# A fused decoder layer on one core: which engine sums, multiplies, normalizes and writes out at the end

## The chip, the core and the metric

The kernel runs on one core of a Trainium2 chip. Its time is the device time of one execution in microseconds (us); the number that counts is the median of the timed executions. Each core has a matrix engine (TensorE, PE in the profile; PEld is its weight load), a vector engine (VectorE, DVE), a scalar engine (ScalarE, ACT), GpSimd (POOL) and SyncE (SP), which here issues nearly all DMAs. Every engine takes its instructions in the order in which the program lists them, and waits at an instruction until the semaphores that it names are set.

## The reference

The input `x` has 4 sequences of 1024 tokens with 512 features. All numbers are 32-bit floats.

```
x = x + gated_self_attention(layernorm(x))     # 16 heads of 32; softmax, gated per query and key, renormalized
x = x + cross_attention(layernorm(x), ctx)     # 16 heads of 32; keys and values from 1024 tokens of 384 features
x = x + ffn(layernorm(x))                      # 512 -> 64, each of the 64 through its own 16-unit relu network, 64 -> 512
```

Softmax is `exp(s) / sum(exp(s))`. The kernel forms `exp(s)` unnormalized, sums `exp(s) * v` and `exp(s)` separately, and multiplies the first by the reciprocal of the second at the end. The layernorm has no weights: it is `(x - mean) * rs` with `rs = 1 / sqrt(var + eps)`.

## The kernel before

**Units.** The work is cut into 8 units: u = 0 to 3 are self-attention (`ph == 0`) on the four sequences, u = 4 to 7 are cross-attention (`ph == 1`). The last unit is u = 7. A unit has two halves (`hf`) of 512 queries, a half has four groups (`g`) of four heads, and a group has eight steps (`kt`), one for each 128 keys. `attention(u, hf)` makes the 32 steps of a half.

**A step.** `scores` multiplies keys by queries (L623) into PSUM and ScalarE takes the exponential (L629) into two tiles `e`, each of two heads by 512 queries (128x1024). There are six `e` buffers, so three steps are in flight. VectorE then adds the tiles of the eight steps into `es` (L646 for the first sum, L648 for the others). After that the step before is finished: `times` multiplies `e` by the values into the PSUM tile `av` (L671).

**Two ways to the sums of exponentials.** Where `shared` holds, VectorE adds only the first of a step's two `e` tiles, and TensorE sums the second with a column of ones into the PSUM tile `sm` (L679, at each odd step for two steps). Where it does not hold, VectorE adds both tiles and TensorE has no L679. `shared` holds in the self-attention units and in the last unit; units 4 to 6 do without it.

**The end of a group.** `normalize` copies `av` (L688), and with `shared` also `sm` (L690), into the single buffer `both`. One step later `add_up` sums the partitions of `es` by ones (L701), ScalarE copies the result (L702), and SyncE writes it to memory and reads it back in another layout (L707 to L717). `divide` forms the reciprocals (L738), writes them to memory (L741) and reads them back broadcast as `recb` (L745). `multiply` (L751) multiplies `both` by `recb` into the query tile `q`. `after(steps, f, behind)` sets the step: in the last unit `divide` comes three steps after `add_up` and `multiply` three steps after that, so a group's `multiply` is in step 7 of the next group. With `behind` the call comes after that step's scores and additions, without it ahead of them. The next group's `av` copy needs `both`, so it needs this `multiply`. The very last group (`closing`) has a path of its own.

**Beside the steps.** `run` spreads other work over the 32 steps by cost. In the last unit (`beside`, branch `u + 1 == n`) the half `hf` carries what follows the half before it: the output projection (`project`, L106, with L845, L849, L850 behind it on VectorE) in groups 0 and 1, the statistics' root on GpSimd (`root`), the normalization into a tile `r2` (`norm`, L319) and its way to memory (`away`, L323) at the start of group 2, the reading back as `xn` (`load_xT`, L328), the 64 inner features (`inputs`, L937), and then the 16 relus (`hidden`). `r2` has two buffers, so the third normalization of a half waits until the first one's rows have been written. Two normalizations follow step 0 of group 2 and two follow step 1. `hidden` forms a relu on VectorE (L989) where `own` holds and on ScalarE (L993) where it does not; the sum over the 16 units is on VectorE (L1000). The outputs (`outputs`) are two products (L1011) each, two additions of the residual on VectorE (L1019) and two DMAs on SyncE (L1021). The projection of the half before, for its first token tile and last group, is placed right after step 7 of group 0.

**Score buffers.** Scores go through two PSUM tiles of two banks and, in the last unit, through two spare banks where nothing else needs them (`score_banks`). So the scores of half a step can start when the exponentials three half steps back are done.

**The tail.** After the last step the program goes on in an order written out by hand: the last group's sums, the projection, the normalization, the feed-forward network and the last four output tiles.

Of the kernel before, what the change touches and what calls it, by code (L numbers as in the profile page):

```python
# [10 lines left out]
F32 = mybir.dt.float32  # L11
# [5 lines left out]
P = 128  # L17
# [51 lines left out]
def moderate_path(tc: tile.TileContext, a: dict, out: bass.AP, flag: bass.AP):  # L69
    nc = tc.nc  # L70
    x = a["x"]
    with ExitStack() as st:
# [527 lines left out]
        def attention(u, hf):  # L600
# [5 lines left out]

            shared = ph == 0 or u + 1 == len(order)

# [6 lines left out]
            def scores(g, kt):  # L615
# [16 lines left out]
                if closing(g):  # L632
# [9 lines left out]
                    return es  # L642
                for i in range(1 if shared else 2):
                    if kt == 1:
                        me.setdefault("es", {})[i] = p1.tile([P, 2, HALF], F32, tag=f"es{i}", name="es")
                        nc.vector.tensor_tensor(me["es"][i], me["e", 0][i], es[i], ALU.add)  # L646
                    elif kt > 1:
                        nc.vector.tensor_tensor(me["es"][i], me["es"][i], es[i], ALU.add)  # L648
# [19 lines left out]
            def times(g, kt, es):  # L668
                for h in range(HG):
                    r = slice(h * DH, (h + 1) * DH)  # L670
                    nc.tensor.matmul(  # L671
                        av[r, :], lhsT=me["v"][:, kt, HG * g + h, :], rhs=es[h // 2][:, h % 2, :],
                        start=(kt == 0), stop=(kt == NT - 1),
                    )
                if shared and kt % 2 and not closing(g):

                    for j in range(4):
                        t, h = kt - 1 + j // 2, j % 2
                        nc.tensor.matmul(  # L679
                            sm[j * DH : j * DH + sums, :],  # L680
                            lhsT=me["sw"][:, t, HG * g + 2 + h, :] if ph == 0 else ones, rhs=me["e", t][1][:, h, :],
                            start=(kt == 1), stop=(kt == NT - 1),
                        )

            def normalize(g):
                i = (u * 2 + hf) * HG + g
                both = p1.tile([P, 3, HALF], F32, tag="both", name="both")
                nc.scalar.copy(both[:, 0, :], av)  # L688
                if shared:
                    nc.scalar.copy(both[:, 1, :], sm)  # L690
# [7 lines left out]
            def add_up(g, i, both, added):  # L698
# [8 lines left out]
                nc.sync.dma_start(s1[0:n], rows[0:n, 0, 2, :])  # L707
                if not shared:
                    nc.sync.dma_start(c[:, 0, 0, :], s1[0:n].rearrange("h (q e) -> (h q) e", e=INNER))
# [12 lines left out]
            def divide(g, i, both, c):  # L722
                if shared:
                    both_ = p2.tile([P, sums, INNER], F32, tag="c2", name="both_")
                    nc.vector.tensor_tensor(both_, c[:, 0:sums, 0, :], c[:, 0:sums, 1, :], ALU.add)
                else:
                    both_ = c[:, 0:1, 0, :]
# [16 lines left out]
                for j in range(HG):  # L744
                    nc.sync.dma_start(  # L745
                        all_[j * DH : (j + 1) * DH, :], rec_d[i % 4][j : j + 1, :].to_broadcast([DH, HALF])
                    )
                after(apart(g), lambda: multiply(g, both, all_), behind=u + 1 < len(order))

# [51 lines left out]
        def post(u, hf):  # L801
# [65 lines left out]
            def root(a=0, n=4):  # L867
# [4 lines left out]
                for t in range(n):  # L872
                    res["rs", a + t] = rs[:, t : t + 1]
                res["rs all"] = rs

            def shift():
# [24 lines left out]
            def norm(t):  # L901
                def f():
# [9 lines left out]
                    r2 = p2.tile([P, 1, D], F32, tag="r2", name="r2")  # L912
                    normalized(r2[:, 0, :], res[t], res["mv"], res["rs", t], t)
                    away(rows_d[b][hf], r2, t, 1)
# [67 lines left out]
            def hidden(h):  # L982
                def f():

                    own = u + 1 < n
                    if h < INNER:
# [20 lines left out]
            def outputs(t):  # L1007
# [8 lines left out]
                def add():  # L1016
                    for k in range(2):
                        i = 2 * k + t
                        nc.vector.tensor_tensor(res[i], res["po", t][k], res[i], ALU.add)  # L1019
                        tt = 4 * hf + i  # L1020
                        nc.sync.dma_start(out[b][tt * P : (tt + 1) * P, :], res[i])  # L1021
# [847 lines left out]
```

## Time and profile before

| what | us |
|---|---|
| median of 3 timed runs | 2163.8 |
| lowest and highest of them | 2163.7, 2164.66 |
| the profiled execution's own time | 2166.25 |
| its span, from first to last instruction | 2164.4 |
| TensorE busy | 2145.8 (99%) |
| VectorE busy | 1503.4 (69%) |
| ScalarE busy | 1233.1 (57%) |
| GpSimd busy | 133.0 (6%) |

The profile page gives the busy time of each engine, the chain of work that ended last, and groups of instructions by line and shape with their mean duration. The trace behind it answers questions: what waited for what, the instructions of one engine in order of time, and the busy time of each engine in a stretch. A time such as 2084.6 is counted from the first instruction. In a line of the timeline the columns are start, duration, engine, line, operation, output and inputs, shapes and count; a bracket gives the idle time of the engine before it and what ended it. The last unit's steps run from about 1918 to 2126 us.

### The profile page before, as it was taken

The page shows a single profiled execution, that of the slowest core. Times are in us where ns is not written, and L with a number is a line of the kernel's source. Part 1 is how long each engine was busy: PE and PEld are TensorE (multiplying, and loading weights), DVE is VectorE, ACT ScalarE, POOL GpSimd, SP SyncE. Part 2 cuts the span into 40 slices and gives each one's busy share as a digit, 9 for nine tenths or more (in the row PEclk, how much of TensorE's full clock was granted, in tenths as well). Part 3 has the DMA queues.
Part 4 walks back from the last instruction along what each step waited for, and adds up shares of the span by engine and source line. Part 5 has one row for each costly group of instructions (what it writes and reads, how often), then busy time and mean ns, then how long its engine had stood idle before and what let it go on. Part 6 is the DMA issues. An engine that isn't in the chain of part 4 may idle for free.

```text
span 2164.4 us, 52976 instructions
## 1 busy us (share of the span) xinstructions
PE 2145.8 (99%) x22792; PEld 555.9 (26%) x22792; DVE 1503.4 (69%) x2251; ACT 1233.1 (57%) x1495; POOL 133.0 (6%) x182
## 2 busy tenths in 40 slices
PE   9999999999999999999999999999999999999998
PEld 4322222222222222222222222222222222222223
DVE  3477675786766866657667666787878868876656
ACT  0156545655556554565666666565655566566765
POOL 2000010040120100001000010000000000000001
PEclk9999999999999999999999999999999999999999
DMA  6412134032331221211322113322423122322231
GB/s 169 122 47 68 52 100 114 19 87 69 90 109 34 81 59 53 68 48 65 71 71 79 63 59 69 96 66 71 89 80 102 63 61 57 98 60 71 71 90 47
DMA packets 154136, 161.71 MB, mean 75 GB/s; under 512 B 47002, under 2 KB 92698, under 8 KB 152740
## 3 DMA queue, kind: packets, MB, share of 16 engines
q1 hardware_dynamic: 149828, 156.14, 25.9%
q8 instruction: 180, 2.95, 0.6%
q0 software_dynamic: 2080, 0.98, 0.3%
q10 hardware_dynamic: 1984, 1.12, 0.2%
q14 instruction: 64, 0.52, 0.1%
HBM read 115.40 MB, written 42.74 MB: 73 GB/s over the span
## 4 chain that ended last, share of the span: by engine, by line
PE 97%; DVE 1%; ACT 1%; issue 1%; DMA 0%; SPq 0%; POOL 0%; DVEq 0%; ACTq 0%
PE f L106 37%; PE s L623 24%; PE av L671 23%; PE sm L679 6%; PE sm L701 3%; PE s L106 1%; PE f L937 1%; ACT e L629 1%; PE f L623 0%; PE f L1011 0%; DMA xin<-in_x 0%; PE f L498 0%; DVE res L1019 0%; PE f L971 0%; DVE es L648 0%
## 5 line engine op out<-in xcount | busy, mean ns | idle before, releaser
L629 ACT ACTIVATE e<-s 128x1024 f32<-128x1024 f32 x997 | 969.4, 1023 | 715.7 <-PE s L623 509.1
L648 DVE TENSOR_TENSOR es<-es,e 128x1024 f32<-128x1024 f32 x522 | 628.4, 1227 | 259.2 <-ACT e L629 258.4
L623 PE MATMUL s<-q,k 32*64 32x512 f32 x7976 | 583.6, 613 | 0.5 <-ACT e L629 0.4
L671 PE MATMUL av<-e,v 128*32 128x512 f32 x4096 | 551.6, 604 | 0.0
L106 PE MATMUL f<-xT,w 128*32 128x512 f32 x2816 | 333.7, 592 | 0.0
L656 DVE SCALAR_TENSOR_TENSOR eg<-e,sw,eg 128x512 f32<-128x512 f32 x448 | 315.6, 746 | 9.3 <-ACT eg L655 9.3
L646 DVE TENSOR_TENSOR es<-e 128x1024 f32<-128x1024 f32 x87 | 104.4, 1223 | 213.4 <-ACT e L629 202.6
L106 PE MATMUL f<-w,q 128*32 128x512 f32 x1984 | 238.6, 593 | 2.0 <-DVE res L845 1.8
L623 PEld LDWEIGHTS s<-q,k 32*64 32x64 f32 x7976 | 127.0, 129 | 412.4 <-ACT e L629 201.6
L671 PEld LDWEIGHTS av<-e,v 128*32 128x32 f32 x4096 | 88.4, 108 | 403.4 <-issue 403.0
L106 PEld LDWEIGHTS f<-xT,w 128*32 128x32 f32 x2816 | 92.2, 110 | 210.4 <-issue 208.0
L679 PE MATMUL sm<-e,sw 128*2 128x512 f32 x1024 | 133.3, 592 | 0.0
L106 PE MATMUL f<-w,xT 128*32 128x512 f32 x896 | 106.0, 592 | 0.6 <-DVE q L308 0.6
L106 PEld LDWEIGHTS f<-w,q 128*32 128x32 f32 x1984 | 64.9, 110 | 152.1 <-issue 143.2
L106 PE MATMUL f<-w,ctxT 128*32 128x512 f32 x768 | 92.3, 592 | 0.0
L106 PE MATMUL f<-ctxT,w 128*32 128x512 f32 x768 | 92.3, 592 | 0.0
L853 POOL TENSOR_TENSOR r<-res,bo_bc 128x512 f32<-128x512 f32 x32 | 40.9, 1278 | 759.4 <-DVE res L845 613.2
L701 PE MATMUL sm<-es,fixed 128*1 128x512 f32 x348 | 66.1, 596 | 3.5 <-ACT both L690 3.3
L314 POOL TENSOR_SCALAR rs<-fmv 128x4 f32<-128x4 f32 (+2 forms) x18 | 10.1, 562 | 854.8 <-DVE fmv L850 854.8
L845 DVE TENSOR_TENSOR res<-f,res 128x512 f32<-128x512 f32 x62 | 42.6, 687 | 27.7 <-PE f L106 15.0
L1000 DVE SCALAR_TENSOR_TENSOR g<-hid,units,g 128x256 f32<-128x256 f32 x105 | 50.3, 479 | 0.9 <-ACT hid L993 0.2
L751 DVE TENSOR_TENSOR q<-both,recb 128x512 f32<-128x512 f32 x63 | 43.2, 686 | 8.5 <-DMA recb<-rec_d 8.5
(285 smaller groups left out, 1185.6 us busy)
## 6 DMA issues: line engine op xcount, KB each, us to landing
recb<-rec_d SPq DMA_DIRECT2D x252, 64.0 KB
xT<-rows_d SPq DMA_DIRECT2D x60, 256.0 KB
rows_d<-r SPq DMA_DIRECT2D x60, 256.0 KB
w<-in_xattn_Wo SPq DMA_DIRECT2D x9, 1024.0 KB
w<-wout_d SPq DMA_DIRECT2D x8, 1024.0 KB
res<-in_x SPq DMA_DIRECT2D x32, 256.0 KB
x1b_d<-r SPq DMA_DIRECT2D x32, 256.0 KB
res<-x1b_d SPq DMA_DIRECT2D x32, 256.0 KB
```

The lines of the kernel that those rows point to most:

```text
L106: nc.tensor.matmul(to[r], lhsT=lhsT[:, j, :] if len(lhsT.shape) == 3 else lhsT[:, r], rhs=rhs, **flags)
L623: nc.tensor.matmul(two[j][m : m + 64], lhsT=k[r, g, kt * P + m : kt * P + m + 64], rhs=q[r, g, :], start=True, stop=True,)
L629: nc.scalar.activation(e[:, h, :] if len(reads) == 1 else e[:, h.start, :], s, AF.Exp, scale=SCALE)
L646: nc.vector.tensor_tensor(me["es"][i], me["e", 0][i], es[i], ALU.add)
L648: nc.vector.tensor_tensor(me["es"][i], me["es"][i], es[i], ALU.add)
L656: nc.vector.scalar_tensor_tensor(eg, es[0][:, h, :], gate(kt), eg, ALU.mult, ALU.add)
L671: nc.tensor.matmul(av[r, :], lhsT=me["v"][:, kt, HG * g + h, :], rhs=es[h // 2][:, h % 2, :], start=(kt == 0), stop=(kt == NT - 1),)
L679: nc.tensor.matmul(sm[j * DH : j * DH + sums, :], lhsT=me["sw"][:, t, HG * g + 2 + h, :] if ph == 0 else ones, rhs=me["e", t][1][:, h, :], ...
L701: nc.tensor.matmul(sm[j * DH : j * DH + 1, :], lhsT=ones, rhs=e, start=True, stop=True)
L751: nc.vector.tensor_tensor(me["q", hf][:, g, :], both[:, 0, :], all_, ALU.mult)
L845: nc.vector.tensor_tensor(r, res["po"], r, ALU.add)
L1000: nc.vector.scalar_tensor_tensor(res["g"], res["hid"], units[:, 2, h - 1 : h], res["g"], ALU.mult, ALU.add)
```

## The change

It has five parts.

1. In the last unit, group 1 of each half is no longer `shared`: VectorE adds both `e` tiles, the L679 products and the L690 copy go, `add_up` has four products in place of two, and the way through memory has two DMAs in place of four.
2. In the last unit `multiply` comes behind the scores and additions of its step.
3. In units 4 to 7, except for the last half, ScalarE normalizes the tokens in place of VectorE, with a shift `nm = -mean * rs` that GpSimd forms by two more instructions.
4. The relus of unit 6's second half go from VectorE to ScalarE.
5. Of the last four output tiles one is copied out of PSUM by ScalarE, added by GpSimd and written by a DMA that ScalarE issues.

```diff
--- before.py
+++ after.py
@@ -604,7 +604,8 @@
             steps = []
             sums = 2 if ph == 0 else 1
 
-            shared = ph == 0 or u + 1 == len(order)
+            def shared(g):
+                return ph == 0 or (u + 1 == len(order) and not (g == 1))
 
             def apart(g):
                 return 2 if u + 1 < len(order) else 3
@@ -640,7 +641,7 @@
                     if kt == 3:
                         after(2, lambda: by_ones(me["first"], True, False), behind=True)
                     return es
-                for i in range(1 if shared else 2):
+                for i in range(1 if shared(g) else 2):
                     if kt == 1:
                         me.setdefault("es", {})[i] = p1.tile([P, 2, HALF], F32, tag=f"es{i}", name="es")
                         nc.vector.tensor_tensor(me["es"][i], me["e", 0][i], es[i], ALU.add)
@@ -672,7 +673,7 @@
                         av[r, :], lhsT=me["v"][:, kt, HG * g + h, :], rhs=es[h // 2][:, h % 2, :],
                         start=(kt == 0), stop=(kt == NT - 1),
                     )
-                if shared and kt % 2 and not closing(g):
+                if shared(g) and kt % 2 and not closing(g):
 
                     for j in range(4):
                         t, h = kt - 1 + j // 2, j % 2
@@ -686,7 +687,7 @@
                 i = (u * 2 + hf) * HG + g
                 both = p1.tile([P, 3, HALF], F32, tag="both", name="both")
                 nc.scalar.copy(both[:, 0, :], av)
-                if shared:
+                if shared(g):
                     nc.scalar.copy(both[:, 1, :], sm)
                     added = [me["es"][0][:, 0, :], me["es"][0][:, 1, :]]
                     if ph == 0:
@@ -705,7 +706,7 @@
                 rows = both.rearrange("(j r) s q -> j r s q", r=DH)
                 n = len(added)
                 nc.sync.dma_start(s1[0:n], rows[0:n, 0, 2, :])
-                if not shared:
+                if not shared(g):
                     nc.sync.dma_start(c[:, 0, 0, :], s1[0:n].rearrange("h (q e) -> (h q) e", e=INNER))
                 else:
                     for k in range(sums):
@@ -720,7 +721,7 @@
                 after(apart(g), lambda: divide(g, i, both, c))
 
             def divide(g, i, both, c):
-                if shared:
+                if shared(g):
                     both_ = p2.tile([P, sums, INNER], F32, tag="c2", name="both_")
                     nc.vector.tensor_tensor(both_, c[:, 0:sums, 0, :], c[:, 0:sums, 1, :], ALU.add)
                 else:
@@ -745,7 +746,7 @@
                     nc.sync.dma_start(
                         all_[j * DH : (j + 1) * DH, :], rec_d[i % 4][j : j + 1, :].to_broadcast([DH, HALF])
                     )
-                after(apart(g), lambda: multiply(g, both, all_), behind=u + 1 < len(order))
+                after(apart(g), lambda: multiply(g, both, all_), behind=True)
 
             def multiply(g, both, all_):
                 nc.vector.tensor_tensor(me["q", hf][:, g, :], both[:, 0, :], all_, ALU.mult)
@@ -872,6 +873,10 @@
                 for t in range(n):
                     res["rs", a + t] = rs[:, t : t + 1]
                 res["rs all"] = rs
+                if ph == 1 and not last:
+                    nm = res["nm"] = p2.tile([P, n], F32, tag="ve", name="nm")
+                    nc.gpsimd.tensor_tensor(nm, res["mv"][:, a : a + n, 0], rs, ALU.mult)
+                    nc.gpsimd.tensor_scalar(nm, nm, -1.0, None, ALU.mult)
 
             def shift():
                 nm = res["nm"] = p2.tile([P, 2], F32, tag="ve", name="nm")
@@ -910,7 +915,10 @@
                             normalized(to, res[t], res["mv"], res["rs", t], t)
                         return
                     r2 = p2.tile([P, 1, D], F32, tag="r2", name="r2")
-                    normalized(r2[:, 0, :], res[t], res["mv"], res["rs", t], t)
+                    if ph == 1:
+                        nc.scalar.activation(r2[:, 0, :], res[t], AF.Identity, bias=res["nm"][:, t : t + 1], scale=res["rs", t])
+                    else:
+                        normalized(r2[:, 0, :], res[t], res["mv"], res["rs", t], t)
                     away(rows_d[b][hf], r2, t, 1)
                 return [(0, f)]
 
@@ -982,7 +990,7 @@
             def hidden(h):
                 def f():
 
-                    own = u + 1 < n
+                    own = u + 1 < n and (u + 2 < n or hf == 0)
                     if h < INNER:
                         hid = p2.tile([P, 2 * P], F32, tag="hid", name="hid")
                     if own and h < INNER:
@@ -1016,8 +1024,14 @@
                 def add():
                     for k in range(2):
                         i = 2 * k + t
+                        tt = 4 * hf + i
+                        if last and i == 2:
+                            r2 = p2.tile([P, D], F32, tag="r2", name="r2")
+                            nc.scalar.copy(r2, res["po", t][k])
+                            nc.gpsimd.tensor_tensor(res[i], r2, res[i], ALU.add)
+                            nc.scalar.dma_start(out[b][tt * P : (tt + 1) * P, :], res[i])
+                            continue
                         nc.vector.tensor_tensor(res[i], res["po", t][k], res[i], ALU.add)
-                        tt = 4 * hf + i
                         nc.sync.dma_start(out[b][tt * P : (tt + 1) * P, :], res[i])
 
                 def f():
```

## The prediction

> **What bounds the kernel now.** I read the page's busy times first, then the waits of TensorE, then the last unit's groups in a table of stretches, then the instructions around the one long wait.
>
> ```profile
> PE 2145.8 (99%) x22792; PEld 555.9 (26%) x22792; DVE 1503.4 (69%) x2251; ACT 1233.1 (57%) x1495; POOL 133.0 (6%) x182
> ```
>
> TensorE is the bound. Work taken off it counts, work taken off VectorE counts only where TensorE waits for VectorE. Its waits add up to little (columns: total, times, longest):
>
> ```profile
> PE sm L701 <- ACT both L690: 3.3, 2, 2.1
> ```
>
> Both are at the start of a half's group 3: 1.24 us at 1999.4 and 2.05 us at 2102.9. The stretches (busy time and count of each engine; PEclk is the granted clock) are group 1 of the first half, groups 1 and 2 of the second, and 3.3 us behind the longer wait:
>
> ```profile
> 1941.00:1974.00 33.00, 33.00 (x337) 8.00 (x340) 22.66 (x42) 16.98 (x19) 1.55 (x3) 1.00 0.08 26
> ...
> 2043.70:2076.70 33.00, 33.00 (x336) 7.99 (x340) 17.02 (x27) 20.43 (x31) 1.55 (x3) 1.00 0.09 26
> 2076.70:2101.70 25.00, 24.06 (x262) 5.25 (x260) 15.12 (x24) 19.29 (x28) 0.00 (x0) 1.00 0.59 161
> 2102.90:2106.20 3.30, 3.30 (x16) 0.83 (x18) 1.80 (x3) 2.29 (x3) 0.00 (x0) 0.50 0.00 0
> ```
>
> In group 1 VectorE has 10 to 16 us free and ScalarE 13 to 16. In group 2 ScalarE is the busier one. The last line: after a wait of 2.05 us TensorE ran at half clock for 3.4 us, which costs another 1.7.
>
> **Part 1, TensorE's gain.** The products by ones in group 1 (start, duration):
>
> ```profile
> 2076.64 1.06 PE L671 MATMUL av<-e,v 128*32 128x512 f32 x8
> 2077.52 1.04 PE L679 MATMUL sm<-e,fixed 128*1 128x512 f32 x8
> 2078.49 0.66 PE L623 MATMUL f<-q,k 32*64 32x512 f32 x4
> ```
>
> From L671 to the scores behind it are 1.85 us; without L679 (2073.51 to 2074.51) it is 1.00. So L679 costs 0.85 us, four times a group: 3.4 us in each of two groups, 6.8 in all. The two further products of L701 run in columns of the array that are idle beside the two of now: nothing.
>
> **Part 1, VectorE's cost.** 7 more additions in a group at 1.15 us (two in 2.35) are 8.05 us. They fit into the free time, but not at its end. Walking VectorE's list from step 5 of group 1 in the second half, with TensorE 0.85 us earlier for each L679 gone: the additions of step 6 end at 2071.35, the first output pair (L1019, 1.2 us) at 2072.55, the additions of step 7 at 2074.85, `multiply` (now behind them, 0.62) at 2075.45, the second output pair at 2076.65. Before it was 2077.02. So TensorE's 2.5 us up to here shrink to 0.4 on the path through VectorE to the output DMAs, and SyncE issues the rest behind those.
>
> **Part 3 in group 2 of the second half.** The lines on which the forecast rests:
>
> ```profile
> 2077.52 1.89 SPq L820 DMA_DIRECT2D res<-x1b_d  x4
> 2079.51 0.85 SPq L323 DMA_DIRECT2D rows_d<-r  x2
> ...
> 2082.65 1.02 ACT L629 ACTIVATE e<-s 128x1024 f32<-128x1024 f32 x1 [0.50 <-PE f L623]
> ...
> 2084.62 1.19 DVE L319 TENSOR_SCALAR r<-res,fmv,rs 128x512 f32<-128x512 f32 x2 [2.58 <-DMA rows_d<-r]
> ...
> 2097.42 1.71 SPq L745 DMA_DIRECT2D recb<-rec_d  x4
> 2100.91 0.69 DVE L751 TENSOR_TENSOR q<-both,recb 128x512 f32<-128x512 f32 x1 [1.70 <-DMA recb<-rec_d]
> 2101.68 0.59 ACT L688 COPY both<-av 128x512 f32<-128x512 f32 x1 [1.88 <-PE s L623]
> 2102.88 1.02 PE L701 MATMUL sm<-es,fixed 128*1 128x512 f32 x2 [2.05 <-ACT both L690]
> ```
>
> The third normalization waited 2.58 us on VectorE for its `r2` buffer, whose rows were issued at 2079.51, behind four loads of 256 KB, and had landed at 2084.5: 5 us. On VectorE nobody minded. On ScalarE the exponentials of step 2 (2082.65) stand behind it. New times: `av` copy 2076.7; two normalizations of 0.75 (L908, the same operation in the tail: two in 1.52) to 2078.2; exponentials of step 1 to 2080.2; L702 to 2080.8. The rows are issued at 2079.1, land 5 us later, so ScalarE stands from 2080.8 to 2084.15. The third and fourth normalization end at 2085.65, the exponentials of step 2 at 2087.6. TensorE gets half of the scores of step 3 out by 2082.7, then waits for the first of these exponentials (2086.65); its values product of step 2 starts at 2087.65, against 2085.44 before. The 3.4 us are gone and 2.2 more.
>
> But the end of group 2 had slack of the other kind. There the last four lines are the chain: `recb` lands, `multiply` frees `both`, the copies follow, L701 starts at 2102.88. In the new program the rows of the later two normalizations are issued at 2085.0 (before: 2086.69), and everything down to `recb` comes 1.3 us earlier, so TensorE is no longer held there. It needs 15.4 us from the product of step 2 to the end of the scores ahead of L701 (2085.44 to 2100.83), which puts L701 at 2103.05. A wait of 4 us should halve the clock for 3.4 us as the 2.05 us did; TensorE works for some 2.6 of these, a loss of 1.3: 2104.35. Before, the same half-clock stretch came behind 2102.88, so the place to compare with is 2102.88 + 1.7 = 2104.58. Sum for this half: -0.2 us.
>
> [...]
>
> **The same in the first half.** There no loads stand ahead of the rows (issued 1975.58), and `xn` loads show a landing 2.3 us after issue (1983.2 to 1985.55). VectorE's second output pair ends at 1975.55 (before 1974.4), `multiply` at 1974.35, so the `av` copy waits until 1974.4 and TensorE 0.35 us for it. The two pairs of normalizations put the exponentials of step 2 at 1980.6 to 1982.6, and the product of step 2 starts at 1982.65, against 1982.75: the 3.4 us are lost here as well, in waits of at most 1 us. The reciprocals' chain then comes 1.0 us earlier, `multiply` ends at 1997.0 in place of 1998.0, and L701 starts at 1998.25 in place of 1999.38. Sum: -1.2 us (1.1 and the 0.1).
>
> **Part 2.** Ahead of the additions, a `multiply` that waits for `recb` holds them; behind them it holds nothing. At the end of group 2 it buys nothing, since L701 waits for the copies too. At the end of group 0 of the second half it costs:
>
> ```profile
> 2039.29 0.68 DVE L751 TENSOR_TENSOR q<-both,recb 128x512 f32<-128x512 f32 x1
> 2040.75 1.90 PE L106 MATMUL f<-w,q 128*32 128x512 f32 x16
> 2041.03 1.22 DVE L648 TENSOR_TENSOR es<-es,e 128x1024 f32<-128x1024 f32 x1 [1.06 <-ACT e L629]
> ```
>
> The second half of those 16 products (from 2041.6) reads the `q` that L751 writes. Behind the addition L751 ends at 2042.85: TensorE waits 1.25 us, call it +1.3.
>
> **Part 4.** 16 relus leave VectorE, which has room here, for ScalarE at 0.5 us apiece (L993: 605 ns, overlapped by 0.1). They fall one to two in a step from 2003 to 2038, where ScalarE's idle time is 3.7 us in group 3 (five gaps) and 2.5 us in group 0 up to step 5, for 4 and 3 us of relus and 1.8 of copies that it has anyway. Step by step the `sm` copy ahead of L701 of group 0 ends at 2022.95 in place of 2022.2, and TensorE keeps this loss: +0.8. Bounds 0 (as in the second half's group 3, where relus already are on ScalarE and TensorE waited only 0.18) and 1.7 (all relus beyond the idle time).
>
> **Part 3 in units 4 to 6.** Five halves. TensorE leaves 1.0 to 2.0 us of idle in ScalarE's step there, and a normalization is 0.75. Twice (root ending at 1504.3 and at 1750.3) ScalarE comes to the first one before GpSimd has `nm`: a wait to about 1751.2 with two small instructions at 0.35 behind the copy. The exponentials then end at 1753.9 and TensorE needs them at 1754.12. I take +0.2 for all; bounds 0 and 1.5 (GpSimd's small operations reach 1.1).
>
> **Part 5.** Four additions from 2155.28 to 2157.76 become three, to 2157.1. The fourth tile goes by a copy (0.6) and a GpSimd addition (1.28, as L881): 2157.2. I take -0.5, bounds 0 and -0.7. It lies on the path to the end.
>
> **The sum** against the profiled execution (span 2164.4, own time 2166.25; its span is near the timed runs' median of 2163.8, to which I apply the difference): -1.2 + 0.8 + 1.3 - 0.2 + 0.2 - 0.5 = +0.4 us, so 2164.2.
>
> **Rivals.** (a) The cover holds: rows land 2.3 us after issue in the second half too, or ScalarE's queue lags less than I walked. Then the 6.8 us stay, both waits at the start of group 3 go (3.3) and with them the half-clock stretch (1.7), less 2.1 for parts 2 and 4 and 0.5 from the tail: 2163.8 - 6.8 - 3.3 - 1.7 + 2.1 - 0.5 = 2153.6. Half of it, 2158.7, is what one half gives. For it: only the second half shows a wait for `r2`, and in units 4 to 6 none did. Against: the loads of 1 MB ahead of those rows do not change.
>
> (b) Slower: rows in the first half land after 5 us as well, because the four output DMAs, 256 KB each, now lie closer to them. ScalarE then stands until 1981.1, the product of step 2 starts at 1984.65 (+1.9), the wait of 2.6 us halves the clock there too (+1.7), and L701 comes at 2.3 us behind its place of now, in place of 1.1 ahead, with the full 1.7 for the clock in the second half (+0.4 more): 2164.2 + 3.5 + 0.4 = 2168.1, and each further 0.5 us of landing adds as much. It decides from a landing of some 3 us. Against: the row of the first half shows a normalization at 1979.26 without a wait.
>
> (c) The change does less than it says: additions and norms only move, no wait appears or goes beyond the L679 saving, and the tail: 2163.8 - 6.8 - 0.5 = 2156.5. Both long waits would stay where they are; that needs the chain through memory to move with TensorE, which the walk denies.
>
> **How the numbers follow.** A measurement of this kernel can tell about 0.2% from no change, 4.3 us: faster is below 2159.5, slower above 2168.1. Forecast (within a few us of now) 0.62; (a) with its half and (c) 0.24; (b) and worse, such as ScalarE becoming the bound in group 3, 0.14. The range leaves out a tenth on each side: 2157.0 to 2168.5.
>
> **What would show it.** Right: L679 and L690 absent in group 1; L908-like normalizations on ScalarE with an idle gap of 2 to 4 us near 2081 to 2084 released by `rows_d`; TensorE waiting for exponentials there and PEclk 0.5 behind it; the wait at L701 gone; a wait of about 1.3 us of L106 for `q` near 2042; a slightly shorter end. Wrong: no such gap on ScalarE, group 1 and group 2 of a half together 3 us shorter or more.

## The result, and the profile after

The change makes the kernel slower: 2171.29 us median of 9 runs (2168.57 to 2172.6) against 2164.16 us for the kernel before, also 9 runs (2162.47 to 2166.54). The ratio is 1.0031, interval 1.0021 to 1.0041. The forecast was 2164.2 us, with a range up to 2168.5: the time lies outside it, on the slow side.

The profiled execution of the kernel after has a span of 2170.5 us (before 2164.4). The page's line of busy times:

```profile
PE 2146.5 (99%) x22736; PEld 553.4 (25%) x22736; DVE 1500.4 (69%) x2218; ACT 1258.5 (58%) x1538; POOL 142.0 (7%) x197
```

TensorE has 56 matmuls fewer on record and is still busy 0.7 us longer. The products by ones were taken out: group 1 has 1.6 us less in the first half and 2.2 in the second. The busy time came back in group 2 of the second half (3.1 us, where the clock is halved), in group 3 of the first (1.9) and in units 4 to 6 (1.4). ScalarE has 25 us more, GpSimd 9. In TensorE's waits (total, times, longest) the 3.3 us at the start of a half's group 3 have shrunk to 0.3, and two new waits have come in elsewhere:

```profile
PE s L624 <- ACT e L630: 3.1, 3, 2.8
...
PE f L106 <- DVE q L752: 1.1, 1, 1.1
...
PE sm L702 <- ACT both L691: 0.3, 1, 0.3
```

The table of stretches (busy time and count of PE, PEld, DVE, ACT, POOL, then PEclk, DMA share, GB/s) for group 1 of the first half, groups 1 and 2 of the second half, and the half-clock stretch:

```profile
1942.30:1974.20 31.90, 31.27 (x310) 7.92 (x308) 28.01 (x47) 16.96 (x19) 4.34 (x5) 1.00 0.07 23
2046.00:2077.10 31.10, 31.07 (x316) 7.66 (x308) 22.99 (x32) 20.44 (x31) 4.34 (x5) 1.00 0.08 26
2077.10:2106.90 29.80, 26.74 (x252) 5.39 (x240) 16.52 (x23) 20.51 (x29) 0.00 (x0) 0.89 0.48 135
2089.80:2096.60 6.80, 6.80 (x44) 1.03 (x40) 4.21 (x8) 4.12 (x6) 0.00 (x0) 0.50 0.84 159
```

Group 1 got shorter: 31.1 us for 33.0 in the second half. Group 2 of the second half got longer, with 3 us in which TensorE stands and 6.8 at half clock, where before it was 25.0 us with 0.9 idle. The reason is on ScalarE (start, duration, and in brackets the idle time ahead with its releaser; the first line is of unit 5, the last of the tail):

```profile
1505.46 0.81 ACT L919 ACTIVATE r<-res,nm,rs 128x512 f32<-128x512 f32 x1 [2.45 <-POOL nm L879]
...
2080.10 1.53 ACT L919 ACTIVATE r<-res,nm,rs 128x512 f32<-128x512 f32 x2
...
2086.88 1.52 ACT L919 ACTIVATE r<-res,nm,rs 128x512 f32<-128x512 f32 x2 [2.88 <-DMA rows_d<-r]
2088.30 1.00 ACT L630 ACTIVATE e<-s 128x1024 f32<-128x1024 f32 x1
...
2160.26 0.59 ACT L1030 COPY r<-s 128x512 f32<-128x512 f32 x1 [4.30 <-DVE res L1034]
```

The second pair of normalizations stands 2.88 us until the rows of the first pair have left, and the exponentials of step 2 stand behind it. SyncE's queue shows why the rows are late: they are issued at 2082.03 behind the four residual loads.

```profile
2080.03 1.90 SPq L821 DMA_DIRECT2D res<-x1b_d  x4
2082.03 0.85 SPq L323 DMA_DIRECT2D rows_d<-r  x2
...
2087.72 1.02 SPq L323 DMA_DIRECT2D rows_d<-r  x2
2090.55 1.93 SPq L328 DMA_DIRECT2D xn<-rows_d  x4
```

TensorE's own instructions show the two new waits, for the `q` of part 2 and for the late exponentials. Its matmuls take twice as long behind the second: eight of L672 took 1.06 us at 2083.67 and 1.94 at 2090.93.

```profile
2044.53 1.06 PE L106 MATMUL f<-w,q 128*32 128x512 f32 x8 [1.13 <-DVE q L752]
...
2083.67 1.06 PE L672 MATMUL av<-e,v 128*32 128x512 f32 x8
...
2089.36 1.65 PE L624 MATMUL s<-q,k 32*64 32x512 f32 x8 [2.75 <-ACT e L630]
2090.93 1.94 PE L672 MATMUL av<-e,v 128*32 128x512 f32 x8
```

Last, the program's closing instructions. Each engine ends with a DRAIN. The columns are the count, the shortest, median and longest duration in ns, and the first and last start. Kernel after:

```profile
L1879 POOLq DRAIN  x3: 46/107/5052, 2164.6 to 2170.3; - x3
L1879 SPq DRAIN  x3: 7/7/13, 2167.9 to 2170.0; - x3
```

Kernel before:

```profile
L1865 POOLq DRAIN  x3: 46/107/5052, 2154.5 to 2164.1; - x3
L1865 SPq DRAIN  x3: 7/7/13, 2163.5 to 2163.8; - x3
```

GpSimd's first drain takes 5.05 us in both. Before, it ran from 2154.5 to 2159.6 while SyncE still waited for the output DMAs until 2163.5: hidden. After, GpSimd has the last output's addition, its drain starts at 2164.6 and ends at 2169.7, 1.8 us behind SyncE's 2167.9.

**The time by stages.** The start of ScalarE's copy of `av` marks the end of each group. Set against before, less the 0.33 us that the two profiles differ at the first such copy, the shifts at the end of each stage are: 1.41 us at the end of unit 6, still 1.41 after group 0 of the last unit's first half, 0.52 after group 2, 1.26 after group 3, 2.62 after group 0 of the second half, 0.76 after group 1, 5.64 after group 2, 3.92 at the start of the tail and 5.83 at the end. The later sections use the same marks.

They compare one execution of each kernel, and the executions of one kernel differ. The two spans are 6.1 us apart, the medians 7.1: the profiled execution before (2166.25 us) is one of the longer ones.

### The profile page after: what moved, and what is told of

It reads as the page before. It is cut to its first block, busy times and chain, and to the rows that moved or that the text cites. A ratio compares the mean times of both kernels' runs of the same rounds, so it can differ in the third digit from the quotient of the medians.

```text
span 2170.5 us, 52906 instructions
## 1 busy us (share of the span) xinstructions
PE 2146.5 (99%) x22736; PEld 553.4 (25%) x22736; DVE 1500.4 (69%) x2218; ACT 1258.5 (58%) x1538; POOL 142.0 (7%) x197
## 5 line engine op out<-in xcount | busy, mean ns | idle before, releaser
L649 DVE TENSOR_TENSOR es<-es,e 128x1024 f32<-128x1024 f32 x534 | 641.9, 1227 | 277.6 <-ACT e L630 276.4
L624 PE MATMUL s<-q,k 32*64 32x512 f32 x7976 | 588.4, 613 | 3.3 <-ACT e L630 3.1
L672 PE MATMUL av<-e,v 128*32 128x512 f32 x4096 | 550.0, 605 | 0.0
L624 PEld LDWEIGHTS s<-q,k 32*64 32x64 f32 x7976 | 127.7, 129 | 418.5 <-ACT e L630 211.8
L672 PEld LDWEIGHTS av<-e,v 128*32 128x32 f32 x4096 | 87.9, 108 | 404.4 <-issue 403.4
L846 DVE TENSOR_TENSOR res<-f,res 128x512 f32<-128x512 f32 x62 | 42.5, 686 | 24.6 <-PE f L106 18.2
L680 PEld LDWEIGHTS sm<-e,sw 128*2 128x2 f32 x1024 | 26.9, 85 | 79.8 <-issue 79.8
```

Of the source, the lines that this page charges most:

```text
L624: nc.tensor.matmul(two[j][m : m + 64], lhsT=k[r, g, kt * P + m : kt * P + m + 64], rhs=q[r, g, :], start=True, stop=True,)
L672: nc.tensor.matmul(av[r, :], lhsT=me["v"][:, kt, HG * g + h, :], rhs=es[h // 2][:, h % 2, :], start=(kt == 0), stop=(kt == NT - 1),)
L680: nc.tensor.matmul(sm[j * DH : j * DH + sums, :], lhsT=me["sw"][:, t, HG * g + 2 + h, :] if ph == 0 else ones, rhs=me["e", t][1][:, h, :], ...
L846: nc.vector.tensor_tensor(r, res["po"], r, ALU.add)
```

## The experiments

Each median stands with its ratio to the runs of the kernel before on the same chip (medians 2164.4 to 2165.0 there); 0.001 of the ratio is 2.2 us. The ratio need not be the quotient of the two medians. Runs of different sets stand on different chips, on which the kernel before differs by up to 0.9 us. A first set undoes one part of the change each time.

**Part 5 undone.**
```
-                        if last and i == 2:
+                        if False:
```


> The changed kernel with part 5 undone: all four last additions on VectorE, all four DMAs on SyncE. Theory: GpSimd's last instruction comes late, so its closing drain (5.05 us in both profiles, 2154.5 to 2159.6 before, 2164.7 to 2169.7 in the changed kernel) now ends last, 1.8 us behind SyncE's; undone, the drain is hidden again and the end comes 1.5 to 1.9 us earlier, 1.0 us of this after the copy and the GpSimd addition that no longer shorten VectorE's row of additions is taken off: 1.3 to 1.9 us faster than the changed kernel. Rival: the drain does not matter and part 5 gains the predicted 0.5 us, so undoing it is 0.5 us slower.

2169.57 us, ratio 1.0019 (1.0010 to 1.0028), some 2 us better than the whole change, though the two intervals overlap. In its profile GpSimd's long drain runs from 2158.4 to 2163.4, ahead of SyncE's at 2166.9, and the stretch from the start of the tail to the end is 0.3 us shorter than before, where the whole change has it 1.9 longer. Part 5 costs 2.2 us by this, of which the drains show 1.8.

**Part 3 undone** (VectorE normalizes as before).
```
-                if ph == 1 and not last:
+                if False:
...
-                    if ph == 1:
+                    if False:
```


> The changed kernel with part 3 undone: VectorE normalizes, GpSimd forms no shift. Theory: ScalarE's two waits for the shift (2.4 us each, 0.7 us on TensorE each) and its wait of 2.9 us for the rows in group 2 of the second half go, TensorE does not wait 2.75 us there, and the half clock does not come at that place; the wait of L702 for the copies of both at the start of group 3 comes back with 1 to 2 us and may halve the clock there. 3 to 4.5 us faster than the changed kernel. Rival: group 2's wait only changes places with the one at L702, so 1.4 us (the two shifts) is all.

2170.6 us, 1.0027 (1.0016 to 1.0038): far less of a gain than expected. The waits for `nm` in units 4 to 6 are gone (their end is at +0.24, with the change +1.41), ScalarE's wait for rows too. But TensorE now waits at the start of group 3:

```profile
PE sm L702 <- ACT both L691: 4.4, 2, 4.1
```

Half clock follows from 2103.95 for 3.4 us. By the marks group 2 of the second half is 2.1 us longer than before, against 4.9 with part 3. One wait stands in for another; which is taken up below.

**Part 2 undone** (the product ahead of the additions in the last unit).
```
-                after(apart(g), lambda: multiply(g, both, all_), behind=True)
+                after(apart(g), lambda: multiply(g, both, all_), behind=u + 1 < len(order))
```


> The changed kernel with part 2 undone: the product by reciprocals ahead of its step's scores and additions. Theory: TensorE's wait of 1.1 us for q at the end of group 0 of the second half goes, and the copy of av in group 2 comes earlier, which buys nothing behind ScalarE's wait: 0.8 to 1.3 us faster. Rival: ahead of the additions it holds them up for its row of reciprocals and VectorE's lag in group 1 grows: 0 to 1 us slower.

2170.8 us, 1.0025 (1.0015 to 1.0034). Group 0 of the second half shifts by 0.02 in place of 1.36 us: that step is right. The median is 0.5 us below the whole change's, which the intervals don't settle. The half-clock stretch lasts 3.4 us in this profile in place of 6.8. The profiled execution is one of four at 2167.0 to 2168.8 us; the other six took 2170.7 to 2172.4, and how long their clock was halved isn't on record.

**Part 4 undone** (all relus of that half on VectorE).
```
-                    own = u + 1 < n and (u + 2 < n or hf == 0)
+                    own = u + 1 < n
```


> The changed kernel with part 4 undone: the 16 relus of unit 6's second half on VectorE. Theory: group 3 of the first half and group 0 of the second lose 0.7 to 1 us less, so 0.5 to 1.2 us faster. Rival: VectorE needs that room for the further additions and the time stays within 0.3 us or grows.

2171.47 us, 1.0031 (1.0019 to 1.0043). In the profile group 3 of the first half shifts by -0.05 in place of +0.74, as it should. The median shows nothing of it; the span of this profile is 1.4 us below that of the whole change, half of it in this group and half in units 4 to 6, where the two programs are the same. A step of this size is not settled by the medians.

**Part 1 alone**, on the kernel before.
```
-            shared = ph == 0 or u + 1 == len(order)
+            def shared(g):
+                return ph == 0 or (u + 1 == len(order) and not (g == 1))
```


> Part 1 alone on the kernel before: group 1's sums on VectorE, all else as before. Theory: TensorE gains 0.65 us up to the end of group 1 of the first half and 1.86 us in the second (what the profiles of the changed kernel and of the runs with one part undone show), some more at the start of group 3 of the first half, and the chain through memory (reciprocals, their row, the product, the copy of av) holds the second half where it was before: 1 to 2.5 us faster than before, with the wait of L702 and the half clock behind it still there. Rival, the plain count of products: 6.8 us faster.

2160.34 us, 0.9977 (0.9968 to 0.9986): faster than before, by 4.1 us of the medians (3.0 to 6.9 by the interval). Against the profile of before the last unit takes 6.5 us less: 1.9 in groups 1 and 2 of the first half, 2.9 in those of the second, 1.7 because no half-clock stretch follows. TensorE's wait at the start of the second half's group 3 is 1.1 us. Unit 5 is 1.3 us longer in this profile, by a half-clock stretch behind a wait of 2.1 us. The 6.5 us are not the worth of the products by ones alone: they hold that half-clock stretch and the waits at the start of group 3, and not every execution of the kernel before has them as long. Of its 27 runs beside this one, 17 had a mean clock of 0.999 and a median of 2164.14 us, ten had 0.998 or 0.997 and 2165.85; the profiled execution has 0.998. A mean of 0.999 leaves at most 6.5 us at half clock, and the tail alone takes 3.5 in the profile before (from 2160.90 to its end) and 5.7 in that of the kernel after (from 2164.85), so by this estimate those 17 had no such stretch of 3.41 us ahead of it. The profile of the late GpSimd instruction below, the same program up to its last addition, has none either. Set against that profile, the last unit gains 3.8 us up to the end of group 2 of the second half, which fits the 4.1. Of the plain count of 6.8 us some 4 are there.

**The loads behind the `xn` loads**, on the kernel after: the rows get a free queue.
```
-                out += (ending[0]["load"] if hf else []) + weave(last["ln"], pause(5)) + last["xT"]
+                out += weave(last["ln"], pause(5)) + last["xT"] + (ending[0]["load"] if hf else [])
```


> The changed kernel, but the four residual loads of the tail (1 MB) go on SyncE's queue behind the reading back of xn, not ahead of the normalized rows. Theory: in the second half the rows are issued 1.9 us earlier and land some 2.3 us after issue, as in the first half, so ScalarE's wait of 2.9 us, TensorE's of 2.75 us and the 6.8 us at half clock go; group 2 of the second half then loses about what it loses in the first, and the time falls by 4 to 6 us against the changed kernel. Rival: ScalarE's own work in group 2 (four normalizations, 3 us) is what delays TensorE, and the time falls by less than 1.5 us.

2173.55 us, 1.0040 (1.0026 to 1.0053): no better than the whole change (the intervals overlap). ScalarE's wait for rows in the second half is gone. But the four loads now stand ahead of `rec_d` and `recb` in SyncE's queue (loads from 2091.13, `rec_d` at 2094.49, `recb` at 2101.26), and the copies at the start of group 3 wait for them:

```profile
PE sm L702 <- ACT both L691: 5.1, 2, 4.9
```

**Part 1 and that place of the loads**, on the kernel before.

> Part 1 with the residual loads behind the reading back of xn, none of the other parts. Theory: the rows and with them the whole chain through memory come about 2 us or more earlier in the second half, so the wait of L702 there shrinks or goes, and with it perhaps the half clock: 3 to 6 us faster than before. Rival: the loads then collide with the reading back of xn and the reciprocals and the wait at L702 stays: 1 to 2.5 us faster, as part 1 alone.

2163.15 us, 0.9993 (0.9984 to 1.0002). The same place costs here too: all eleven runs lie above the eleven of part 1 alone on this chip, the copies hold TensorE 3.1 us, and the clock is halved for 6.8 us from 2099.35, still within the wait.

**A late GpSimd instruction**, on the kernel before: a copy of 128x1 behind the last addition, for nothing but to start GpSimd's drain late.
```
+        nc.gpsimd.tensor_copy(marks[:, 0:1], tail["res"][3][:, 0:1])
```


> The kernel before with one small GpSimd instruction (128x1) behind the last addition of the output, nothing else changed. Theory: its closing drain of 5.05 us starts only after it and ends last: 1.7 to 2.5 us slower than before. Rival: the drain's length is the wait for others, so it shrinks to the remaining time and nothing changes (within 0.5 us).

2168.49 us, 1.0020 (1.0011 to 1.0029), 4.1 us over before for a copy of 0.18 us. The drains in its profile:

```profile
L1866 POOLq DRAIN  x3: 46/107/5052, 2160.3 to 2165.9; - x3
L1866 SPq DRAIN  x3: 7/7/13, 2161.6 to 2165.6; - x3
```

GpSimd's long one starts at 2160.3, so it ends at 2165.4, 3.8 us behind SyncE's. The cost of the drain is shown by itself. It starts 4.7 us after the copy has ended (2155.60), in the kernel after 2.5 us after the addition; what it waits for until then the profiles don't show.

**The loads behind the reciprocals' last transfer**, with part 1 alone.
```
-                out += (ending[0]["load"] if hf else []) + weave(last["ln"], pause(5)) + last["xT"]
+                out += weave(last["ln"], pause(5)) + last["xT"]
                 out += weave(last["b"], pause(8))
-                out += weave(last["tr"], pause(3)) + pause(2) + last["s"] + weave(some(last, 8), pause(12))
+                out += weave(last["tr"], pause(3)) + (ending[0]["load"] if hf else []) + pause(2) + last["s"] + weave(some(last, 8), pause(12))
```


> The kernel before with part 1 alone, and the four residual loads of the second half (256 KB each) moved behind the reciprocals' last transfer, so that they stand neither ahead of the rows nor ahead of rec_d and recb. Theory (part 1 is worth its plain count, and the loads cost only what is queued behind them): rows land some 2.5 to 3 us after issue in place of 5, no half-clock stretch in the last unit, 2157 to 2160 us, at or below the 2160.3 of part 1 alone. Rival (the loads only change place and hold the next thing in SyncE's queue, the softmax sums of group 3): TensorE waits 3 us or more behind group 3, and the time is 2162 or more.

2159.15 us, 0.9970 (0.9959 to 0.9980): the fastest kernel of this study, faster than both before and after. SyncE's queue in its profile:

```profile
2076.61 0.89 SPq L323 DMA_DIRECT2D rows_d<-r  x2
...
2081.44 0.86 SPq L323 DMA_DIRECT2D rows_d<-r  x2
2084.31 1.93 SPq L328 DMA_DIRECT2D xn<-rows_d  x4
...
2092.36 1.71 SPq L746 DMA_DIRECT2D recb<-rec_d  x4
2094.11 1.85 SPq L821 DMA_DIRECT2D res<-x1b_d  x4
```

The second rows are followed by the `xn` loads, which wait for them, after 2.9 us; the loads go last and hold nobody. No wait for the copies is left at the start of group 3, and in the last unit the clock is full up to the tail. (In unit 5 this execution has a half-clock stretch of 3.41 us from 1612.88, which costs it 1.1 us by the marks.) Whether it beats part 1 alone the intervals don't settle: they overlap.

**Part 3 added to that**, with `nm` by one VectorE instruction.
```
-                    nc.gpsimd.tensor_tensor(nm, res["mv"][:, a : a + n, 0], rs, ALU.mult)
-                    nc.gpsimd.tensor_scalar(nm, nm, -1.0, None, ALU.mult)
+                    nc.vector.scalar_tensor_tensor(nm, res["mv"][:, a : a + n, 0], -1.0, rs, ALU.mult, ALU.mult)
```


> The run before this one with part 3 as well: the cross tokens normalized on ScalarE, with nm formed by one VectorE instruction so that the nm waits of units 4 to 6 can't come in. Theory (part 3 costs only because the rows land late, and its nm on GpSimd): with the rows landing early ScalarE has no gap by rows_d above 1 us, and the time is within 1.5 us of the run without part 3. Rival (normalizations on ScalarE cost in themselves, since ScalarE is the busier engine of group 2): 3 us or more slower than the run without part 3, with TensorE waiting for ScalarE's exponentials in group 2.

2163.95 us, 0.9994 (0.9985 to 1.0003), 4.8 above the run without part 3. ScalarE has no gap by `rows_d` above 0.64 us in the last unit, as the theory had it, but the time is the rival's. By the marks of the two profiles 2.9 us lie in units 4 to 6 (4.0 without the half-clock stretch that the other run has there) and 2.5 in the last unit, where the normalizations stand between ScalarE's exponentials (group 2 of the two halves is 1.5 and 0.9 longer). In unit 5, where `nm` from GpSimd made ScalarE wait 2.45 us, the waits are now two (L918 there is L919 above):

```profile
1504.34 0.81 ACT L918 ACTIVATE r<-res,nm,rs 128x512 f32<-128x512 f32 x1 [0.94 <-DVE nm L878]
...
1510.12 0.81 ACT L918 ACTIVATE r<-res,nm,rs 128x512 f32<-128x512 f32 x1 [1.72 <-DMA rows_d<-r]
```

`nm` comes earlier, and the second pair of normalizations meets its rows before they have landed. Part 3 has a price without late rows in the last unit as well.

**Parts 1 and 2**, loads at their place of before.

> The kernel before with parts 1 and 2: as part 1 alone, with the product by reciprocals behind the additions. Theory (part 2 costs 1.3 us in group 0 of the second half and nothing else): 2161.6, that is 1.3 above part 1 alone, and the wait of the L702 products for the copies near 2100 stays at about 1 us. Rival (behind the additions the product also frees the sums later and holds the chain through memory, which explains the 4 us wait in the run with part 3 undone): that wait is 3 to 4 us and a half-clock stretch follows it, 2164 to 2166.

2162.04 us, 0.9991 (0.9982 to 1.0000): 0.4 above the theory's 2161.6. Group 0 of the second half shifts by 1.33 us, the wait for the copies is 0.9.

**Parts 1 and 3**, loads at their place of before, `nm` by VectorE.

> The kernel before with parts 1 and 3, nm formed by one VectorE instruction, the residual loads at their place of before. Theory (ScalarE's stand of some 3 us for the rows halves the clock, and this is what turned part 1's gain into a loss): ScalarE waits about 3 us for rows_d near 2082 to 2086, half clock behind it for 3.4 to 6.8 us, 2164 to 2167, some 5 us above part 1 alone. Rival (part 3 in the last unit is harmless without parts 2 and 4): within 1.5 us of part 1 alone, 2159 to 2162.

2169.27 us, 1.0019 (1.0010 to 1.0028): 8.9 us over part 1 alone, more than the theory's 5.

```profile
2085.59 1.52 ACT L918 ACTIVATE r<-res,nm,rs 128x512 f32<-128x512 f32 x2 [2.40 <-DMA rows_d<-r]
```

ScalarE stands for the rows, TensorE waits 2.3 us for the exponentials, and the clock is halved from 2087.43 for 6.8 us. Against part 1 alone group 2 of the second half is 5.1 us longer, units 4 to 6 and group 2 of the first half 1.3 each. With the loads last, the same part costs 4.8: the late rows and what follows them are some 4 us.

**Parts 1, 2 and 4; parts 1, 2 and 5.** The prices did not add up: the change without part 3 stood at 2170.6, 8.6 us above parts 1 and 2.

> The kernel before with parts 1, 2 and 4. Theory (part 4 moves ScalarE and the second half's transfers against each other, so that the rows land late and hold group 3): rows land 4 us or more after issue near 2086, TensorE waits 3 to 4 us for the copies behind group 2, half clock after it, 2166 to 2168. Rival (part 4 costs its 0.8 us and no more; the rest is part 5's): no such wait, 2162.5 to 2163.5.

2167.66 us, 1.0012 (1.0003 to 1.0021). Its wait:

```profile
PE sm L702 <- ACT both L691: 5.2, 2, 4.9
```

> The kernel before with parts 1, 2 and 5. Theory (part 5 costs the 2 us at the end that GpSimd's closing drain gives, and nothing ahead of it): 2164 to 2165, group 2 of the second half as with parts 1 and 2. Rival (part 5 is what brings the further 6 us, also ahead of the tail): 2168 or more.

2166.13 us, 1.0004 (0.9995 to 1.0013). Its wait:

```profile
PE sm L702 <- ACT both L691: 3.7, 1, 3.7
```

So both have it: it comes without part 4, and it comes without part 5. What the runs share is the landing of the second rows, read from their issue to that of the `xn` loads: 2.9 us with part 1 alone and with parts 1 and 2 (wait for the copies 1.1 and 0.9), 5.2 and 4.7 in these two, 4.8 with part 3 undone (wait 4.9, 3.7 and 4.1). In the three runs with the loads last it was 2.9 each time. In these profiles, with the loads ahead of the rows, the chain through memory has one of two lengths. The timed runs speak against a fixed property of a program: of the eleven of parts 1 and 2, eight took 2161.4 to 2162.5 us and three 2165.7 to 2166.0, with none between, and the profiled execution is one of the eight; those of parts 1, 2 and 5 lie between 2164.1 and 2169.4. That the longer executions are those with the late rows isn't shown, and what decides between the two lengths stays open.

**The whole change, loads last.** The edit of part 1 with late loads, on the kernel after.

> The kernel after with the four residual loads of the second half behind the reciprocals' last transfer. Theory (the rows' landing behind the loads, and the clock that follows, is some 5 us of the loss; parts 2, 4, 5 and the normalizations' own time stay): 2164 to 2167, no half-clock stretch in group 2, ScalarE not held by rows_d by more than 1 us. Rival (what makes the rows late is not the loads): ScalarE or the copies hold TensorE by 2 us or more still, 2169 to 2172.

2166.18 us, 1.0006 (0.9997 to 1.0015): 5.1 below the whole change. ScalarE does not wait for `rows_d` in the second half, the clock is full up to the tail, and what is left of TensorE's waits in the last unit is small:

```profile
PE f L106 <- DVE q L752: 1.1, 1, 1.1
...
PE s L624 <- ACT e L630: 0.7, 3, 0.3
```

Part 1 with the same loads is 7.0 us faster (2159.15). By the marks these are 0.5 us in units 4 to 6 (1.6 here, 1.1 there by the half-clock stretch in unit 5), 1.3 in groups 1 and 2 of the first half and 1.0 in those of the second (part 3), 0.8 (part 4), 1.4 (part 2) and 2.1 at the end (part 5): 7.1.

## Why the prediction was wrong

Its sum by steps, and what the marks show:

| step | predicted, us | measured, us |
|---|---|---|
| groups 1 and 2, first half | -1.2 | -0.9 |
| part 4 | +0.8 | +0.7 |
| part 2 | +1.3 | +1.4 |
| groups 1 to 3, second half | -0.2 | +1.3 |
| part 3 in units 4 to 6 | +0.2 | +1.4 |
| part 5 and the end | -0.5 | +1.9 |
| sum | +0.4 | +5.8 |

**Right.** Four steps stand as walked. The two further products by ones at the end of group 1 cost no time: from the first of them to the scores behind the product by the values are 1.82 us with two (before, 2079.68 to 2081.50) and 1.82 with four (after, 2080.71 to 2082.53). TensorE waits 1.1 us for the `q` of L752. The relus cost 0.7. The gain in the first half nearly vanishes; TensorE's waits for VectorE's output additions there (0.6 and 0.3 us, L1019 and L624 for L1034) are a little longer than the 0.35 walked. In the second half the mechanism is the one foretold: the normalization that needs their buffer starts 4.85 us after the rows' issue (5 foretold), ScalarE stands 2.88 us for them (3.35), TensorE 2.75 (about 4), the wait at the start of group 3 goes, and the clock halves behind the new wait. The parts 1 and 3 run and the one with the loads last show this chain from both sides: with the loads last ScalarE's wait, TensorE's and the half-clock stretch are all gone.

**Wrong, part 5: the sign.** The step "four additions become three" counted the last addition and the output, and not what GpSimd does when it is through. The last addition ends at 2162.18; at the shift of the tail, 3.92 and 0.33, the one of before would end at 2162.01, so the 0.5 us were not there: the copy waited until VectorE's first addition was done at 2160.2. And GpSimd's drain of 5.05 us, hidden before, became the end: 1.8 us. That it is the drain is shown by the run with a lone late copy (+4.1 us) and by the run with part 5 undone. The bounds, 0 and -0.7, left a loss out; the drain stood in the trace of before.

**Wrong, the clock term in size.** One half-clock stretch of 3.4 us was counted, a loss of 1.3. It lasted 6.83 us with TensorE busy through all of it. The second 3.4 us are a loss of 1.7, and -0.2 and 1.7 make +1.5, against the +1.3 of the table. The profile with part 2 undone has one such stretch and a second half (groups 1 to 3) of -0.8. The prediction also took the half-clock stretch of the kernel before, 1.7 us, as given, and that is a matter of the execution, as the clocks beside part 1 alone show. In the profile of the late GpSimd instruction TensorE waits 1.48 us at that place, with full clock behind it; set against it, groups 1 to 3 of the second half lose 3.5 us in place of 1.3.

**Wrong, `nm`: what TensorE waits for.** The two places were named. ScalarE waits 2.45 and 2.44 us there, and each costs TensorE 0.69; the step took +0.2 for all, inside its own bound of 1.5. The time of `nm` was walked right: at the second place it is ready at 1752.13, and the program stands 1.02 us later there, so 1751.11 for the 1751.2 foretold. The walk compared the exponentials with the product by the values (1754.12), for which they were in time. But the second half of the next scores goes into the PSUM tile that the second exponential reads. Before, and after, at the first place:

```profile
1507.10 1.11 PE L623 MATMUL s<-q,k 32*64 32x512 f32 x16
```

```profile
1506.18 1.92 ACT L630 ACTIVATE e<-s 128x1024 f32<-128x1024 f32 x2
1507.43 1.81 PE L624 MATMUL s<-q,k 32*64 32x512 f32 x16
```

The exponentials end at 1508.10, the second half of the scores starts at 1508.15, and the 16 products take 0.70 us longer. This wait stands in no list of waits, since it falls between products that overlap; it counts as busy time.

These three are 2.4, 1.5 and 1.2 us of the 5.4 that the sum was short; the first half gives the other 0.3.

**The rivals.** The slower one, (b), had its 2168.1 by late rows in the first half. That did not happen. (c), the plain count, fell as a forecast of this change, and of the 6.8 us that it gives part 1 the median shows 4.1 with that part alone (2160.34). Part 1's gain was there, and parts 2 to 5, added with it, cost more than it gave. The chance of "slower" (0.14) was too small since three steps erred to the same side, part 5 beyond its bounds and the clock term without any.

## What to carry to other kernels

Work moved to an idle engine brings its waits along: on the engine it comes from nobody may have stood behind a wait of 2.6 us, on the one it goes to the critical work does. When a program's last instruction moves to another engine, read that engine's closing instructions in the trace of before and ask which cover they lose. Before a chain through memory is relied on, see what stands ahead of it in its queue, and move what isn't urgent behind the whole chain: behind its first link alone it cost more than at the front (2163.15 against 2160.34 with part 1).

## What the runs showed of the hardware

GpSimd's closing drain took 5.05 us in the profiles of before, after, part 5 undone, part 1 alone and the late GpSimd instruction: behind an addition of 1.26 us in the kernel after, and behind a copy of 0.18 us with the late instruction.

The length of TensorE's wait alone did not tell whether the clock halved. Before, a wait of 2.05 us went with 3.41 us at half clock (from 2102.87), in the kernel after one of 2.75 us with 6.83 us (from 2089.76), and one of 3.67 us (parts 1, 2 and 5, from 2098.69) with full speed. At one place of unit 5, where the programs are the same, TensorE waits for L845 (L846 in the changed kernels): 1.80 us in part 1 with the loads last were followed by half clock (3.41 us from 1612.88), 1.82 us in the kernel before (to 1611.35) were not. The run with parts 1, 2 and 5, in stretches of 3.41 us:

```profile
2096.87:2100.29 3.42, 1.82 (x24) 0.23 (x16) 3.00 (x4) 0.78 (x2) 0.00 (x0) 1.00 0.27 77
2100.29:2103.70 3.41, 1.34 (x16) 0.51 (x18) 1.52 (x3) 2.46 (x4) 0.00 (x0) 1.00 0.02 5
2103.70:2107.11 3.41, 3.41 (x54) 1.38 (x52) 2.15 (x2) 1.96 (x5) 0.00 (x0) 1.00 0.01 4
```

The wait is split over two stretches, with TensorE busy 1.82 and 1.34 us, and the granted clock is 1.00 in all three. In the kernel before TensorE was busy for 1.37 us of the 3.41 us ahead of the half clock (2099.46 to 2102.87), in the kernel after for 0.66 us (2086.35 to 2089.76).

In both of these profiles a second half-clock stretch starts in the tail. Its start lies 58.027 us behind that of the first one before (2102.870 and 2160.897), which is 17 times 3.4133 us, and 75.093 us after (2089.760 and 2164.853), 22 times 3.4133 us. The stretches ahead of the tail, 3.41 and 6.83 us, are one and two times that length. Whether the place of a wait between such multiples matters isn't shown. What decides between 1.37 us with half clock and 1.34 without, and between 3.41 us at half clock and 6.83, stays open.
